# A two-layer gated cross-attention kernel: first-stage PSUM as four pairs of banks, a group's three score slots in a row

## The chip, the cores and the metric

One Trainium2 chip, one of its cores. The metric is device microseconds (us) for one launch of the whole program, lower is better. The program computes with TensorE (matrix products, here PE for its matmuls and PEld for its weight loads), VectorE (DVE), ScalarE (ACT) and GpSimd (POOL); SyncE (SP) issues most DMAs. Matrix products land in PSUM, eight banks of 512 float32 values in each of 128 partitions; only DVE and ACT read them out from there.

## The reference

All values are float32. Sixteen sequences `x` of 256 tokens by 256 features pass through two layers, each an attention to a context of 77 tokens and a feed-forward part, each added to `x` through a `tanh` gate:

```python
x = x + tanh(g_xattn[0]) * L0_xattn(ctx, layernorm(x))   # first stage: this change
x = x + tanh(g_ffn[0])   * L0_ffn(layernorm(x))          # second stage: 2 of 8 experts per token
x = x + tanh(g_xattn[1]) * L1_xattn(layernorm(x), ctx)   # third stage
x = x + tanh(g_ffn[1])   * L1_ffn(layernorm(x))          # fourth stage: gated linear attention
```

The first stage, cut to what matters:

```python
xl, l = layer_norm(ctx), layer_norm(layernorm(x))
q     = l @ Wq                                   # 16 heads of 64
k, v  = split(concat([xl, l], axis=1) @ Wkv)     # 256 + 77 = 333 keys
w     = softmax(q k^T / 8)
out   = (w v) merged over heads @ Wo
```

## The kernel before

The program runs the four stages one after the other. A check at the end decides whether a slow exact version is run as well; it isn't here. The change lies in `stage0_fast`, the first stage, and in two small steps of `Route`, the second stage's routing, which runs in between.

**Units.** `stage0_fast` works on 64 units `(b, g)`: 16 sequences, and for each four groups `g` of four heads. The engines follow the written order: the objects `pe`, `act`, `dve` and `pool` go through the class `Pinned`, whose `call` (line 50) keeps every instruction in its engine's program order. So nearly every row of the profile has line 50, and one tells rows apart by their tiles. The order of one unit is written out in the loop over `units`:

- `run(ahead_of, ...)`: small statistics and routing steps.
- `scores(b, g, ahead)`: 333 keys are three chunks of 111 (`KC`), and a group has two head pairs `n`, so there are six blocks. Three slots `sc`, each two banks, take two blocks each: eight matmuls a slot (`sc<-qk`), each over 64 contraction rows, that is half of the array's height, so that the two heads `j` of a pair run side by side. Each slot is followed by one `exp` on ACT (`e<-sc`, 111x1024). Ahead of the third slot, `heads(*ahead, 0)` puts half of the next unit's projections.
- `heads(b, g, n)`: the queries and keys of one head pair, in banks `q` and `k`, with all 128 rows and columns; ACT takes `q` out (`qk<-q`), DVE takes `k` out (`qk<-k`).
- in group 1, `turn(b + 1)` (transposes `tr`, taken out by DVE into `kvT`) and `project(b - 1)` (`proj`, taken out and added to `x` by DVE).
- `sums`: POOL adds the exponentials of the unit over the chunks (`es`) and into a running check (`esum`).
- `values(*behind)`: for the unit before, `den<-es,ones` (the softmax sums) and `o<-e,v`, both as four tiles of 32 columns side by side; then DVE takes the reciprocal (`rd<-den`) and multiplies (`oT<-o,rd`).
- `run(behind_values, ...)`: routing products `rank`, `rtr` (group 2) and `rt` (group 3).
- in group 2, `all_values(b + 1)`: six products `v<-wkv,kvT` of 111x512 per sequence (three chunks by two halves `h`). ACT takes out half 0, DVE half 1, each right behind its half's matmuls in the program.
- `heads(*ahead, 1)`: the other half of the next unit's projections; `tally()`.

**PSUM.** The score slots have a pool of their own (`f0psc`, two slots of two banks); all else takes single banks from a pool of four (`f012ps`, `shared_bank`), which stages 1 and 2 go on using. `Route.logits` and `Route.ranks` leave their 16 and 32 columns in PSUM until a later unit reads them (`exps`, `place`).

Each matmul of the program runs as two passes in the trace, so counts in the profile are double those in the code. A tile that is written again waits for those that still read what it held; the waits are set by the framework from the tiles that instructions touch.

Of the kernel before, what the change touches and what calls it, by code (L numbers as in the profile page):

```python
# [10 lines left out]
F32 = mybir.dt.float32  # L11
I32 = mybir.dt.int32
AF = mybir.ActivationFunctionType
ALU = mybir.AluOpType
AX = mybir.AxisListType
PSUM = bass.MemoryType.PSUM

P = 128
B, S, D = 16, 256, 256
# [54 lines left out]
def layers(ctx: ExitStack, tc: tile.TileContext, t, out, check):  # L74
# [11 lines left out]
    xs, cs = [None] * B, [None] * B  # L86
# [19 lines left out]
    ws1 = s1.enter_context(tc.tile_pool(name="s1w", bufs=1, side="right"))  # L106
# [19 lines left out]
    wo0 = load_w("wo0h" if fast else "wo0", 1024, D, w0)  # L126
# [237 lines left out]
    class Route:  # L364
# [26 lines left out]
        def logits(self, b, bank):  # L391
            ps, xnT = bank("rt"), self.xnT.pop(b)
            for i in range(2):
                for k in range(2):
                    pe.matmul(ps[:, 8 * i:8 * i + 8], xnT[:, k, i * P:(i + 1) * P], rw1[:, k, :],
                              start=k == 0, stop=k == 1)
            self.ps[b] = ps

        def exps(self, b):

# [64 lines left out]
        def ranks(self, b, bank):  # L465
            hs, h1, h2 = self.hs[b]
            ps = bank("rank")
            pe.matmul(ps[:, :16], before, hs[:, 0].rearrange("p i e -> p (i e)"), start=True, stop=True)
            pe.matmul(ps[:, 16:32], ones, hs[:, 1].rearrange("p i e -> p (i e)"), start=True, stop=True)
            self.ps[b] = ps  # L470

        def place(self, b):

# [45 lines left out]
                nc.sync.dma_start(out=by_expert(rows, e),  # L519
                                  in_=bc(zero, [P, n, D], 1))  # L520

    def stage0_fast(bank):
        with ExitStack() as sx:
            w1 = sx.enter_context(tc.tile_pool(name="f0w1", bufs=1, reuse_waits="tile"))
            w2 = sx.enter_context(tc.tile_pool(name="f0w2", bufs=2, reuse_waits="tile"))
            psc = sx.enter_context(tc.tile_pool(name="f0psc", bufs=2, space=PSUM, reuse_waits="tile"))
            esum, rsum = check["esum"], check["rsum0"]

            xn, cn, kvT, v, oT = {}, {}, {}, {}, {}
# [21 lines left out]

            def turn(b):
                kvT[b] = w2.tile([P, 2, NK], F32, tag="kvT", name="kvT")
                for k in range(2):
                    ps = bank("tr")
                    for i in range(2):
                        pe.transpose(ps[:, i * P:(i + 1) * P], xn[b][:, i, k * P:(k + 1) * P], ident)
                    pe.transpose(ps[:, S:NK], cn[b][:, 0, k * P:(k + 1) * P], ident[:S2, :S2])
                    dve.tensor_scalar(kvT[b][:, k, :S], ps[:, :S], vec[:, V_LN2G + k:V_LN2G + k + 1],
                                            vec[:, V_LN2B + k:V_LN2B + k + 1], ALU.mult, ALU.add)  # L560
                    dve.tensor_scalar(kvT[b][:, k, S:], ps[:, S:NK], vec[:, V_LN1G + k:V_LN1G + k + 1],
                                            vec[:, V_LN1B + k:V_LN1B + k + 1], ALU.mult, ALU.add)

            def all_values(b, *between):
                v[b] = w2.tile([KC, 3, 1024], F32, tag="v", name="v")
                for c in range(3):
                    for h in range(2):
                        ps = bank("v")
                        for k in range(2):
                            pe.matmul(ps[:KC, :], kvT[b][:, k, c * KC:(c + 1) * KC],  # L570
                                             wkv0[:, k, 1024 + h * 512:1024 + (h + 1) * 512],
                                             start=k == 0, stop=k == 1)
                        if h == 0:
                            act.copy(v[b][:, c, :512], ps[:KC, :])
                        else:
                            dve.tensor_copy(v[b][:, c, 512:], ps[:KC, :])
                    for x in between[c:c + 1]:
                        x()
# [3 lines left out]
            def heads(b, g, n):  # L582

                if n == 0:
                    qk[b, g] = w2.tile([P, 2, S + NK], F32, tag="qk", name="qk")
                m = 2 * g + n
                psq, psk = bank("q"), bank("k")
                for k in range(2):
                    pe.matmul(psq[:, :S], wq0[:, k, m * P:(m + 1) * P], kvT[b][:, k, :S], start=k == 0, stop=k == 1)
                for k in range(2):  # L590
                    pe.matmul(psk[:, :NK], wkv0[:, k, m * P:(m + 1) * P], kvT[b][:, k, :], start=k == 0, stop=k == 1)
                act.mul(qk[b, g][:, n, :S], psq[:, :S], 0.125)
                dve.tensor_copy(qk[b, g][:, n, S:], psk[:, :NK])

            def scores(b, g, between):

                x_qk = qk.pop((b, g))
                e = w2.tile([KC, 6, 2, S], F32, tag="e", name="e")
                for u in range(0, 6, 2):
                    if u == 4 and between is not None:  # L600
                        heads(*between, 0)
                    sc = psc.tile([P, 2, 2, S], F32, tag="sc", name="sc")
                    for x in range(2):
                        n, c = divmod(u + x, 3)
                        for j in range(2):
                            r = slice(64 * j, 64 * j + 64)
                            pe.matmul(sc[:KC, j, x, :], x_qk[r, n, S + c * KC:S + (c + 1) * KC],
                                             x_qk[r, n, :S], start=True, stop=True)
                    act.activation(e[:, u:u + 2], sc[:KC].rearrange("p j x s -> p x j s"), AF.Exp)
                return b, g, e  # L610
# [10 lines left out]
            def values(b, g, e, es):  # L621

                if g == 0:
                    oT[b] = w1.tile([P, 8, S], F32, tag="oT", name="oT")
                den, ps = bank("den"), bank("o")
                heads = [(h, slice(32 * h, 32 * h + 32)) for h in range(4)]
                for h, r in heads:
                    n, j = divmod(h, 2)
                    pe.matmul(den[r, :S], ones[:KC, :32], es[:, n, j * S:(j + 1) * S], start=True, stop=True)
                for i in range(2):  # L630
                    for c in range(3):
                        for h, r in heads:
                            n, j = divmod(h, 2)
                            lo = (4 * g + h) * 64 + 32 * i
                            pe.matmul(ps[r, i * S:(i + 1) * S], v[b][:, c, lo:lo + 32], e[:, 3 * n + c, j, :],
                                      start=c == 0, stop=c == 2)
                rd = w2.tile([P, S], F32, tag="rd", name="rd")
                dve.reciprocal(rd, den[:, :S])
                dve.tensor_tensor(oT[b][:, 2 * g:2 * g + 2, :], ps.rearrange("p (i s) -> p i s", i=2),
                                  bc(rd, [P, 2, S], 1), ALU.mult)  # L640
                tallies.append((rd, rsum[:, 4 * b + g:4 * b + g + 1]))
# [4 lines left out]
                tallies.clear()  # L646

            def project(b):
                for i in range(2):
                    ps = bank("proj")  # L650
                    for m in range(8):
                        pe.matmul(ps[:, :D], oT[b][:, m, i * P:(i + 1) * P], wo0[:, m, :],
                                         start=m == 0, stop=m == 7)
                    dve.scalar_tensor_tensor(xs[b][:, i, :], ps[:, :D], gate[:, 0:1], xs[b][:, i, :],
                                                   ALU.mult, ALU.add)


            ahead_of = {0: [(norm_y, 1), (route.exps, -2)], 1: [(route.choose, -2)],
# [26 lines left out]
            for n, (b, g) in enumerate(units):  # L685
                ahead = units[n + 1] if n + 1 < len(units) else None
                run(ahead_of, b, g)
                now = scores(b, g, ahead)
                if g == 0 and b + 2 < B:
                    load_c(b + 2)  # L690
                run(behind_scores, b, g)
                if b == 0 and g == 1:
                    clear_rows()
                if g == 1 and b + 1 < B:
                    turn(b + 1)
                if g == 1 and b > 0:
                    project(b - 1)
                now = sums(*now)
                if behind is not None:
                    values(*behind)  # L700
                run(behind_values, b, g)
                if g == 2 and b + 1 < B:
                    all_values(b + 1, *route.weighted(b - 2))
                if ahead is not None:
                    heads(*ahead, 1)
                if g == 2 and b + 1 == B:
                    pieces = route.weighted(b - 2)
# [17 lines left out]
            project(B - 1)  # L725

    if fast:
        s_banks = ctx.enter_context(ExitStack())
        pss = s_banks.enter_context(tc.tile_pool(name="f012ps", bufs=4, space=PSUM, reuse_waits="tile"))

        def shared_bank(name):
            return pss.tile([P, 512], F32, tag="ps", name=name)

        stage0_fast(shared_bank)
    else:
        stage0()
    s0.close()
# [1245 lines left out]
```

## Time and profile before

| what | value |
|---|---|
| time, median of 3 runs | 1972.6 us (1970.68 to 1974.86) |
| the profiled execution | 1979.72 us, span 1977.9 us, mean granted clock 0.988 |
| first stage in the span | up to the first expert matmul at 1004.5 us |
| PE busy in the span | 1936.2 us (98%) |
| PEld, DVE, ACT, POOL busy | 1314.5, 1050.2, 865.7, 1001.3 us |

The profile is one execution, some 7 us above the median of the timed runs. Busy time of PE says little by itself: its matmuls overlap, and the end of each is modelled. What one pass really costs is read from the start of one instruction to the start of the next. In the rows, `sc<-qk 64*111 64x256` reads: result tile `sc` from `qk`, weights of 64 rows by 111 columns, a moving operand of 256 columns.

### The profile page before, as it was taken

To read this page: it belongs to the slowest core of one execution; us is meant where nothing else is said; L and a number is where in the kernel's file an instruction comes from. 1 tells how busy PE (TensorE), PEld (TensorE's weight loads), DVE (VectorE), ACT (ScalarE), POOL (GpSimd) and SP (SyncE) were. 2 spreads that over 40 slices of the span, in tenths; PEclk is the share of its full clock that TensorE was granted. 3 is DMA by queue.
4 is the path that set the end of the run, shared out by engine and by line. 5 is a ranking of instruction groups with operands and counts; after the bars stand their busy time and mean duration, and the time that the engine had idled before them with its cause. 6 is when DMAs were issued, how large, how long until landed. Compare 5 with 4: busy or idle time off the path is not lost.

```text
span 1977.9 us, 35117 instructions
## 1 busy us (share of the span) xinstructions
PE 1936.2 (98%) x13986; PEld 1314.5 (66%) x13986; DVE 1050.2 (53%) x2651; ACT 865.7 (44%) x1763; POOL 1001.3 (51%) x905
## 2 busy tenths in 40 slices
PE   7999999999999999999989999999999999999996
PEld 4666666566665666656677766667777777777775
DVE  3334444444444444444454378866566665666654
ACT  3333334433344333443433478744444444444442
POOL 4544656556565565655634756214444444444433
PEclk9999999999999999999999989999999999999998
DMA  9400000000000000000068823000000000000000
GB/s 333 132 1 3 13 11 13 9 10 11 11 13 10 10 11 9 12 9 9 12 217 238 216 40 49 14 1 6 6 6 7 6 11 6 7 6 9 9 7 13
DMA packets 54013, 75.05 MB, mean 38 GB/s; under 512 B 10080, under 2 KB 43728, under 8 KB 53328
## 3 DMA queue, kind: packets, MB, share of 16 engines
q1 hardware_dynamic: 41552, 55.92, 8.5%
q0 software_dynamic: 12288, 16.79, 4.3%
q8 instruction: 113, 1.85, 0.4%
q14 instruction: 60, 0.49, 0.1%
HBM read 39.14 MB, written 33.55 MB: 37 GB/s over the span
## 4 chain that ended last, share of the span: by engine, by line
PE 95%; DVE 2%; ACT 1%; DMA 1%; POOL 1%; issue 1%; SPq 0%; ACTq 0%; DVEq 0%; POOLq 0%
PE o L50 11%; PE sc L50 11%; PE v L50 9%; PE q L50 8%; PE k L50 8%; PE proj L50 7%; PE kq L1508 6%; PE sc L1508 5%; PE gq L1508 3%; PE proj L1508 3%; PE v L1508 3%; PE ex L50 3%; PE o L1508 3%; PE den L50 2%; PE gz L1508 2%; PE z L1508 2%
## 5 line engine op out<-in xcount | busy, mean ns | idle before, releaser
L50 ACT ACTIVATE e<-sc 111x1024 f32<-111x1024 f32 x192 | 189.3, 1021 | 172.8 <-PE sc L50 172.7
L50 POOL TENSOR_SCALAR rs<-mv 128x2 f32<-128x2 f32 (+1 forms) x96 | 18.4, 192 | 434.3 <-DVE mv L50 431.6
L50 PE MATMUL sc<-qk 64*111 64x256 f32 x1536 | 198.6, 391 | 1.3 <-ACT qk L50 1.0
L50 POOL TENSOR_TENSOR es<-e 111x1024 f32<-111x1024 f32 x64 | 151.3, 2364 | 92.7 <-ACT e L50 92.6
L50 PEld LDWEIGHTS sc<-qk 64*111 64x111 f32 x1536 | 126.7, 172 | 79.0 <-issue 51.5
L50 PE MATMUL o<-e,v 111*32 111x256 f32 x3072 | 178.8, 381 | 0.0
L50 PE MATMUL v<-wkv,kvT 128*111 128x512 f32 x384 | 168.7, 596 | 0.1
L50 DVE COPY qk<-k 128x333 f32<-128x333 f32 x128 | 64.7, 505 | 194.8 <-PE k L50 192.7
L50 POOL TENSOR_TENSOR esum<-esum,es 111x512 f32<-111x512 f32 x128 | 163.0, 1273 | 10.0
L50 PE MATMUL k<-kvT,wkv 128*128 128x333 f32 x512 | 164.4, 443 | 0.0
L50 ACT ACTIVATE qk<-q 128x256 f32<-128x256 f32 x128 | 49.2, 385 | 260.5 <-PE q L50 259.9
L50 POOL TENSOR_TENSOR k<-e,ee 128x256 f32<-128x256 f32 x64 | 46.9, 733 | 223.9 <-ACT e L50 223.9
L50 POOL TENSOR_TENSOR es<-es,e 111x1024 f32<-111x1024 f32 x64 | 150.4, 2350 | 5.0
L50 PEld LDWEIGHTS o<-e,v 111*32 111x32 f32 x3072 | 100.5, 111 | 67.0 <-issue 1.7
L50 PE MATMUL q<-kvT,wq 128*128 128x256 f32 x512 | 142.6, 401 | 0.0
L50 DVE RECIPROCAL rd<-den 128x256 f32<-128x256 f32 x64 | 112.5, 1757 | 54.5 <-PE den L50 52.9
L50 POOL TENSOR_TENSOR at<-at,at 128x768 f32<-128x768 f32 x64 | 115.9, 1811 | 24.8 <-DVE at L50 15.2
L50 PEld LDWEIGHTS v<-wkv,kvT 128*111 128x111 f32 x384 | 66.9, 177 | 90.6 <-issue 86.4
L50 DVE TENSOR_TENSOR at<-sc,amask 128x768 f32<-128x768 f32 x64 | 61.3, 957 | 115.8 <-PE sc L1508 100.4
L50 PEld LDWEIGHTS q<-kvT,wq 128*128 128x128 f32 x512 | 88.2, 189 | 50.0 <-issue 43.2
L50 PEld LDWEIGHTS k<-kvT,wkv 128*128 128x128 f32 x512 | 97.2, 190 | 30.0
L50 POOL DMA_INDIRECT x<-rows_out,pos x64 | 100.4, 1568 | 32.2 <-issue 15.9
(228 smaller groups left out, 4092.4 us busy)
## 6 DMA issues: line engine op xcount, KB each, us to landing
rows<-zero SPq DMA_DIRECT2D x16, 640.0 KB
xin<-rows SPq DMA_DIRECT2D x16, 640.0 KB
rows_out<-y SPq DMA_DIRECT2D x16, 384.0 KB
x<-in_x_dram SPq DMA_DIRECT2D x16, 256.0 KB
rows_out<-y SPq DMA_DIRECT2D x16, 256.0 KB
out_dram<-x SPq DMA_DIRECT2D x16, 256.0 KB
wkv<-in_wkv_dram SPq DMA_DIRECT2D x2, 1024.0 KB
ew<-in_ew_dram SPq DMA_DIRECT2D x2, 1024.0 KB
```

What stands on the lines that cost most here:

```text
L50: x = getattr(self.engine, name)(*a, **k)
L1508: tc.keep_in_program_order(nc.tensor.matmul(*a, **k))
```

## The change

- `stage0_fast` gets a pool of its own, `f0ps`, of four pairs of banks; every step takes a whole pair (`pair`), and `bank` is the first half of one. The shared pool of four banks is made after the stage.
- The three score slots stand one behind the other; `heads(*ahead, 0)` goes to the end of the unit, right ahead of `heads(*ahead, 1)`. `values(*behind)` comes directly behind the scores, and `turn` and `project` behind it.
- `heads`, `values`, `turn`, `project` and `all_values` each put two results into the halves of one pair. `turn` and `project` now run all their matmuls first and take out afterwards, `project` with one DVE instruction in place of two. In `all_values` ACT's copy of half 0 still stands between the matmuls of half 0 and half 1.
- `Route.logits` and `Route.ranks` copy their columns into SBUF with ACT (`copied`), so that no pair is held.

```diff
+            self.copied(b, ps[:, :16])          # logits; ranks: ps[:, :32]
+        def copied(self, b, ps):
+            n = ps.shape[1]
+            self.ps[b] = ws1.tile([P, n], F32, tag=f"copied{n}", name="copied")
+            act.copy(self.ps[b], ps)
...
-            psc = sx.enter_context(tc.tile_pool(name="f0psc", bufs=2, space=PSUM, reuse_waits="tile"))
+            pairs = sx.enter_context(tc.tile_pool(name="f0ps", bufs=4, space=PSUM, reuse_waits="tile"))
+            def pair(name):
+                return pairs.tile([P, 2, 512], F32, tag="ps", name=name)
+            def bank(name):
+                return pair(name)[:, 0, :]
...
             def turn(b):
+                both = pair("tr")
                 for k in range(2):
-                    ps = bank("tr")
+                    ps = both[:, k, :]
                     for i in range(2):
                         pe.transpose(ps[:, i * P:(i + 1) * P], xn[b][:, i, k * P:(k + 1) * P], ident)
                     pe.transpose(ps[:, S:NK], cn[b][:, 0, k * P:(k + 1) * P], ident[:S2, :S2])
+                for k in range(2):
+                    ps = both[:, k, :]
                     dve.tensor_scalar(kvT[b][:, k, :S], ...)
...
             def all_values(b, *between):
                 for c in range(3):
+                    both = pair("v")
                     for h in range(2):
-                        ps = bank("v")
+                        ps = both[:, h, :]
                         for k in range(2):
                             pe.matmul(ps[:KC, :], kvT[b][:, k, c * KC:(c + 1) * KC], ...)
                         if h == 0:
                             act.copy(v[b][:, c, :512], ps[:KC, :])
                         else:
                             dve.tensor_copy(v[b][:, c, 512:], ps[:KC, :])
...
             def heads(b, g, n):
-                psq, psk = bank("q"), bank("k")
+                both = pair("qk")
+                psq, psk = both[:, 0, :], both[:, 1, :]
...
-            def scores(b, g, between):
+            def scores(b, g):
                 for u in range(0, 6, 2):
-                    if u == 4 and between is not None:
-                        heads(*between, 0)
-                    sc = psc.tile([P, 2, 2, S], F32, tag="sc", name="sc")
+                    sc = pair("sc").rearrange("p j (x s) -> p j x s", x=2)
...
             def values(b, g, e, es):
-                den, ps = bank("den"), bank("o")
+                both = pair("o")
+                den, ps = both[:, 0, :], both[:, 1, :]
...
             def project(b):
-                for i in range(2):
-                    ps = bank("proj")
+                both = pair("proj")
+                for i in range(2):
                     for m in range(8):
-                        pe.matmul(ps[:, :D], ...)
-                    dve.scalar_tensor_tensor(xs[b][:, i, :], ps[:, :D], gate[:, 0:1], xs[b][:, i, :], ...)
+                        pe.matmul(both[:, i, :D], ...)
+                dve.scalar_tensor_tensor(xs[b], both[:, :, :D], gate[:, 0:1], xs[b], ALU.mult, ALU.add)
...
-                now = scores(b, g, ahead)
+                now = scores(b, g)
...
+                now = sums(*now)
+                if behind is not None:
+                    values(*behind)
                 if g == 1 and b + 1 < B:
                     turn(b + 1)
                 if g == 1 and b > 0:
                     project(b - 1)
-                now = sums(*now)
-                if behind is not None:
-                    values(*behind)
                 run(behind_values, b, g)
                 if g == 2 and b + 1 < B:
                     all_values(b + 1, *route.weighted(b - 2))
                 if ahead is not None:
+                    heads(*ahead, 0)
                     heads(*ahead, 1)
```

More of the change, by code (lines that the diff above doesn't have):

```diff
@@ L396, in logits @@
                               start=k == 0, stop=k == 1)
-            self.ps[b] = ps
+            self.copied(b, ps[:, :16])
[3 more added lines that the diff above has]
+            act.copy(self.ps[b], ps)
         def exps(self, b):
@@ L469, in ranks @@
             pe.matmul(ps[:, 16:32], ones, hs[:, 1].rearrange("p i e -> p (i e)"), start=True, stop=True)
-            self.ps[b] = ps
+            self.copied(b, ps[:, :32])
         def place(self, b):
@@ L520, in clear_rows, with stage0_fast @@
                                   in_=bc(zero, [P, n, D], 1))
-    def stage0_fast(bank):
+    def stage0_fast():
         with ExitStack() as sx:
@@ L648, in project @@
             def project(b):
+                both = pair("proj")
                 for i in range(2):
-                    ps = bank("proj")
                     for m in range(8):
-                        pe.matmul(ps[:, :D], oT[b][:, m, i * P:(i + 1) * P], wo0[:, m, :],
+                        pe.matmul(both[:, i, :D], oT[b][:, m, i * P:(i + 1) * P], wo0[:, m, :],
                                          start=m == 0, stop=m == 7)
-                    dve.scalar_tensor_tensor(xs[b][:, i, :], ps[:, :D], gate[:, 0:1], xs[b][:, i, :],
-                                                   ALU.mult, ALU.add)
+                dve.scalar_tensor_tensor(xs[b], both[:, :, :D], gate[:, 0:1], xs[b], ALU.mult, ALU.add)
             ahead_of = {0: [(norm_y, 1), (route.exps, -2)], 1: [(route.choose, -2)],
@@ L727, in layers @@
     if fast:
+        stage0_fast()
         s_banks = ctx.enter_context(ExitStack())
@@ L732, in shared_bank @@
             return pss.tile([P, 512], F32, tag="ps", name=name)
-        stage0_fast(shared_bank)
     else:
```

## The prediction

> **What bounds the kernel now.** I read the profile's chain of waits first, to see which engine sets the end.
>
> ```profile
> PE 95%; DVE 2%; ACT 1%; DMA 1%; POOL 1%; issue 1%; SPq 0%; ACTq 0%; DVEq 0%; POOLq 0%
> ```
>
> PE carries it, and the waits between 100 and 950 us name no wait of PE at all, only of the engines that feed on it. So in the first stage each step costs what PE takes from its start to the start of the next, and whatever makes PE wait is added in full. The timeline of PE gives those steps (start, modelled length, passes):
>
> ```profile
> 497.03 1.03 PE L50 MATMUL q<-kvT,wq 128*128 128x256 f32 x4
> 497.90 1.28 PE L50 MATMUL k<-kvT,wkv 128*128 128x333 f32 x4
> ...
> 501.03 1.13 PE L50 MATMUL q<-kvT,wq 128*128 128x256 f32 x4
> 502.00 1.28 PE L50 MATMUL k<-kvT,wkv 128*128 128x333 f32 x4
> 503.21 1.12 PE L50 MATMUL sc<-qk 64*111 64x256 f32 x8
> 504.26 0.64 PE L50 MATMUL den<-es,ones 111*32 111x256 f32 x8
> ...
> 510.49 1.98 PE L50 MATMUL sc<-qk 64*111 64x256 f32 x16
> 512.41 1.13 PE L50 MATMUL q<-kvT,wq 128*128 128x256 f32 x4
> ...
> 957.75 7.17 PE L50 MATMUL proj<-wo0h,oT 128*128 128x256 f32 x32
> 964.85 0.64 PE L50 MATMUL den<-es,ones 111*32 111x256 f32 x8
> ```
>
> The same four `q` passes take 0.87 us behind `v` (497.03 to 497.90, both of the full array) and 0.97 behind scores (501.03 to 502.00). Score passes: x16 take 1.92, x8 take 1.05, so eight cost 0.87 and each run of scores carries 0.18 more, however long it is. PE pays where the shape of its tiles changes.
>
> **The change, part by part.**
>
> *Scores together, heads 0 moved to the unit's end.* One run of 24 passes for runs of 16 and 8 saves one fixed 0.18. The `q` of the second `heads` call now follows `k`, full shape behind full shape: 0.10. The `k` of the first no longer goes over to scores: it took 502.00 to 503.21 = 1.21; the `v` row below gives 10.30 us for 24 passes of 512 columns, 0.84 ns a column, so four passes of 333 are 1.12, and 0.09 goes. Together 0.37 in each of the 63 units that have a next one: 23.3 us.
>
> *Turn and project behind the values.* Before, this block stood alone between scores and `den`. 32 `proj` passes took 957.75 to 964.85 = 7.10, against 32 x 256 x 0.84 ns = 6.87. Behind the values and ahead of `heads` it changes shape no more often than the unit does anyhow: 0.2 x 16 = 3.2 us. Saved in all: **26.5 us**.
>
> *`all_values` with both halves in one pair.* This part decides. The changed program as it is built shows the waits: in every `v` pair the first matmul of half 1 waits for ACT's copy of half 0, since both halves are now one tile and the copy stands ahead of that matmul. Before, the halves were two tiles, and PE ran all 24 passes of a sequence without a break while ACT and DVE took out:
>
> ```profile
> 486.73 10.46 PE L50 MATMUL v<-wkv,kvT 128*111 128x512 f32 x24
> 488.65 0.59 ACT L50 COPY v<-v 111x512 f32<-111x512 f32 x1 [1.13 <-PE v L50]
> ```
>
> 24 passes from 486.73 to 497.03 are 0.43 each. Half 0 is four passes; the fourth starts at 488.02, ends at 488.61 (a `v` pass lasts 0.592) and releases the copy at 488.65. It is done at 489.24. How long PE takes to restart behind ACT, this place shows:
>
> ```profile
> 982.75 1.94 ACT L50 ACTIVATE e<-sc 111x1024 f32<-111x1024 f32 x2 [0.67 <-PE sc L50]
> 983.83 1.12 PE L50 MATMUL sc<-qk 64*111 64x256 f32 x8 [0.32 <-ACT e L50]
> ```
>
> The first of the two `exp` (1.02 each) ends at 983.77, the matmul starts at 983.83: 0.06. So half 1 starts at 489.30 where it started at 488.45: 0.85 late, plus a weight load that nothing covers, 0.10 (the 0.18 of the score run restarted here has to be such a load and the change of shape at its end). 0.95 x 3 pairs x 16 sequences = **45.6 us**. Bounds: 0.85 if the load is covered (40.8), 1.05 if PE needs another 0.1 for the wait (50.4); below nothing is excluded, as the copy cannot start before half 0 ends. Queued behind PE's wait is everything, since PE is the chain. ACT is free for each copy: the two `xw` behind it take 0.91 and the next half 0 ends over 4 us later.
>
> *`heads` in one pair.* ACT's `qk<-q` now waits for the last `k` pass, and DVE's `qk<-k` for ACT: 0.39 + 0.51 + about 0.1 behind the end of `k`. Both are done about 1.5 us after the last `k` pass starts. The first matmul that needs head pair 1 is the seventh of the twelve: 0.37 (change of shape) + 0.95 + 0.43 = 1.75 after it, with its weight load some 0.2 sooner. It just fits: 0. Missed by 0.1 it would cost 63 x 0.1 = 6.3, the upper bound; it cannot gain.
>
> *`values` in one pair.* The reciprocal (1.76) now waits for the last `o` pass, not for `den`, and `oT` (0.69) follows: the pair is free 2.6 us after `o`. PE then has at least the two `heads` (4.2 us) to do, and the next to need that pair is the second score slot. In group 1 `oT` also waits for `project(b - 1)`, which still reads the one `oT` buffer, so DVE stands for 7 us with `kvT`, `x` and both `qk` copies behind it. Afterwards it needs 0.69 + 1.78 + 0.75 + 0.51, done 3.7 us behind `proj`, when PE is still in `heads` (4.2 us). Cover: `heads`. 0.
>
> *`es` on POOL.* `den` comes some 2.6 us sooner behind the scores of the unit before. In the unit at 504 us `es` ended at 510.3 and `den` started at 515.64; 5.3 of slack become 2.7. 0; were it gone, each us would be paid 64 times.
>
> *Copies of 16 and 32 columns, one `x` update for two.* Two small ACT copies a sequence (the small `re<-re` is 0.22) in gaps where ACT waits for PE; DVE's 0.75 (the `128x512` form of that operation later in the run) for 2 x 0.48. Off the chain: 0. SP and POOL issue the same first-stage transfers in the same order; a few loads of the second stage change place on SP, 0 with 1 us either way.
>
> *Start.* The two first `heads` and the first `turn` run with nothing to cover their longer take-out (0.44 and twice 0.2): 0.7 us.
>
> Sum: -26.5 + 45.6 + 0.7 = **+19.8 us**. Against the profiled execution, 1979.7 becomes 1999.5; its time is 7.1 above the median of the timed runs, so the forecast for these is 1972.6 + 19.8 = **1992.4**.
>
> A rule weighed here: the Trainium skill's page "PSUM — Partial Sum Buffer", in its summary of rules, asks only that a reader and a running matmul be in different banks. By it the halves of a pair could go on side by side, and the sum would be -25.8, 1946.8. But the wait is set by tile and is carried in the program, so the trace's durations decide.
>
> **The rivals.**
>
> *Faster: the half-1 wait costs little.* Then the shape changes alone count: 1972.6 - 26.5 + 0.7 = 1946.8. For it: nothing on the chip needs the wait. Against: the copy's 0.59 lies wholly behind half 0. The point of decision is 26.5 / 48 = 0.55 us a half; above that the kernel is slower. I see no way below 0.85. Chance 0.04.
>
> *The clock drops.* An idle PE is given half the clock for a stretch of 3.41 us. Rows of such stretches (length, PE busy and count, weight loads, DVE, ACT, POOL, then the granted clock):
>
> ```profile
> 28.81:32.22 3.41, 2.71 (x20) 2.08 (x21) 1.13 (x5) 2.46 (x5) 0.88 (x2) 1.00 0.99 394
> 32.22:35.63 3.41, 3.41 (x19) 2.21 (x18) 0.64 (x3) 1.61 (x3) 0.00 (x0) 1.00 1.06 337
> 1308.81:1312.22 3.41, 2.37 (x17) 1.75 (x16) 2.45 (x8) 0.75 (x1) 0.28 (x2) 1.00 0.00 0
> 1312.22:1315.64 3.42, 3.42 (x11) 2.76 (x10) 3.16 (x5) 0.00 (x0) 0.61 (x1) 0.50 0.00 0
> 1947.11:1950.52 3.41, 2.55 (x24) 1.77 (x20) 3.23 (x7) 0.95 (x2) 0.73 (x1) 1.00 0.23 79
> 1950.52:1953.93 3.41, 2.96 (x16) 1.73 (x18) 1.83 (x5) 1.89 (x5) 2.61 (x3) 1.00 0.00 0
> ```
>
> 1.04 idle in a stretch brought 0.50 in the next; 0.70 and 0.86 did not. The new gap is 488.61 to 489.30 = 0.69 by the same reckoning, and gaps come 4.4 us apart, so a stretch holds one at most. Below the point, but not by much. If it tips, about 38 of the 48 gaps lie whole in a stretch, each costs half of 3.41: 38 x 1.7 = 65 more, 2057. Chance 0.10. The Trainium skill's "TensorE: Matmul & The Clock Gate" speaks more darkly of this change: under its second failure mode, short idle spells between groups of matmuls, as PSUM banks are cycled, keep the clock swinging, while its table of advice fears only gaps above about 3 us. The first would make it the 2057, the second the 1992.
>
> *No gain from the order.* If the shape changes cost as much in the new places: 1972.6 + 45.6 + 0.7 = 2018.9. Against it: the 0.87 of `q` behind `v`. Chance 0.03.
>
> **How the numbers follow.** The forecast has 0.81, the clock 0.10, no gain 0.03, the faster rival 0.04, a result within 0.2% (about 4 us, what a measurement can tell from no change) 0.02. The forecast's own ends: 40.8 - 30 (0.05 more saved per unit) = +10.8, so 1983; 50.4 + 6.3 + 2 - 23.3 = +35.4, so 2008. Range 1983 to 2008, which leaves out the clock case, no gain and the faster one. Slower: 0.81 + 0.10 + 0.03 = 0.94.
>
> **What would show it.** Right: `sc<-qk` in runs of 24 at about 2.78 us, `q` behind `k` at 0.87; in `v`, a gap of 0.85 to 1.05 after every fourth pass, named as a wait of PE for ACT's `v`, some 33 us idle in all (48 x 0.69); the first expert matmul some 20 us later; clock 1.00 up to there. Wrong: `v` still 10.3 us a sequence; stretches of 0.50 in the `v` phases; waits of `sc` for `qk` or of `den` for `es`.

## The result, and the profile after

| | us, median | ratio to the kernel before, 95% interval |
|---|---|---|
| before, same chip | 1973.7 (1970.68 to 1980.31) | |
| after | 2002.3 (1998.81 to 2008.06) | 1.0143 [1.0106, 1.0180] |
| forecast | 1992.4 (1983 to 2008) | 1.0100 |

The kernel is slower by 28.6 us where 19.8 were forecast. The profiled execution took 2008.06 us, span 2006.3, against 1979.72 and 1977.9 before: 28.4 more. The chain of waits still says that PE sets the end, with 90% where it had 95%:

```profile
PE 90%; DVE 3%; ACT 3%; POOL 2%; issue 1%; DMA 1%; SPq 0%; ACTq 0%; POOLq 0%; DVEq 0%
```

The waits of PE between 100 and 950 us (total, times, longest) were empty before. Now there are two:

```profile
PE v L50 <- ACT v L50: 28.4, 42, 0.7
PE rtr L50 <- ACT rxn L50: 1.2, 2, 1.1
```

42 times is three for each of the 14 sequences in the window. The timeline of PE shows the place, and, some lines further, the shape changes that were saved:

```profile
499.48 1.88 PE L50 MATMUL v<-wkv,kvT 128*111 128x512 f32 x4
502.03 3.69 PE L50 MATMUL v<-wkv,kvT 128*111 128x512 f32 x8 [0.68 <-ACT v L50]
506.40 3.69 PE L50 MATMUL v<-wkv,kvT 128*111 128x512 f32 x8 [0.68 <-ACT v L50]
510.76 1.97 PE L50 MATMUL v<-wkv,kvT 128*111 128x512 f32 x4 [0.68 <-ACT v L50]
512.57 1.03 PE L50 MATMUL qk<-kvT,wq 128*128 128x256 f32 x4
513.43 1.28 PE L50 MATMUL qk<-kvT,wkv 128*128 128x333 f32 x4
514.55 1.02 PE L50 MATMUL qk<-kvT,wq 128*128 128x256 f32 x4
515.41 1.28 PE L50 MATMUL qk<-kvT,wkv 128*128 128x333 f32 x4
516.63 2.85 PE L50 MATMUL sc<-qk 64*111 64x256 f32 x24
519.40 0.64 PE L50 MATMUL o<-es,ones 111*32 111x256 f32 x8
...
544.30 7.11 PE L50 MATMUL proj<-wo0h,oT 128*128 128x256 f32 x32
551.25 1.03 PE L50 MATMUL qk<-kvT,wq 128*128 128x256 f32 x4
```

In program order the 24 passes of a sequence used to be one block of 10.30 us. They are now four blocks with a gap of 0.68 behind every half 0, from 499.48 to 512.57 = 13.09. The 24 score passes are one run, 516.63 to 519.40 = 2.77 (2.78 forecast). `q` behind `k` takes 514.55 to 515.41 = 0.86 (0.87). `proj` takes 6.95 where it took 7.10. What releases each block is ACT's copy:

```profile
501.40 0.58 ACT L50 COPY v<-v 111x512 f32<-111x512 f32 x1 [1.13 <-PE v L50]
501.88 0.91 ACT L50 ACTIVATE xw<-rxn,rw 128x256 f32<-128x256 f32 x2
502.03 0.27 PEld L50 LDWEIGHTS v<-wkv,kvT 128*111 128x111 f32 x2 [1.52 <-ACT v L50]
```

The copy ends at 501.98. The weight load and the matmul of half 1 start at 502.03, 0.05 later. PEld had stood for 1.52: the load waits with its matmul, so nothing covers it.

From sequence to sequence (`v` to `v`, sequences 6 to 15) the kernel takes 62.71 us where it took 61.66, so 1.05 more. That is +2.785 for the three gaps and -1.735 for the order.

### The profile page after: what moved, and what is told of

It is laid out like the page before. It is cut to its first block, busy times and chain, and to the rows that moved or that the text cites. A ratio compares the mean times of both kernels' runs of the same rounds, so it can differ in the third digit from the quotient of the medians.

```text
span 2006.3 us, 34963 instructions
## 1 busy us (share of the span) xinstructions
PE 1925.8 (96%) x13986; PEld 1324.0 (66%) x13986; DVE 1090.7 (54%) x2635; ACT 868.8 (43%) x1795; POOL 1001.5 (50%) x905
## 3 DMA queue, kind: packets, MB, share of 16 engines
q8 instruction: 112, 1.84, 0.4%
## 4 chain that ended last, share of the span: by engine, by line
PE 90%; DVE 3%; ACT 3%; POOL 2%; issue 1%; DMA 1%; SPq 0%; ACTq 0%; POOLq 0%; DVEq 0%
PE o L50 13%; PE qk L50 13%; PE sc L50 10%; PE v L50 9%; PE proj L50 7%; PE kq L1525 6%; PE sc L1525 5%; PE gq L1525 3%; PE proj L1525 3%; PE v L1525 3%; PE o L1525 3%; PE ex L50 2%; PE gz L1525 2%; PE z L1525 2%; PE den L1525 1%; PE q L50 1%
## 5 line engine op out<-in xcount | busy, mean ns | idle before, releaser
L50 PE MATMUL v<-wkv,kvT 128*111 128x512 f32 x384 | 184.2, 617 | 33.1 <-ACT v L50 32.4
L50 ACT ACTIVATE qk<-qk 128x256 f32<-128x256 f32 x128 | 49.1, 384 | 379.5 <-PE qk L50 379.5
L50 ACT ACTIVATE e<-sc 111x1024 f32<-111x1024 f32 x192 | 182.2, 1021 | 17.8 <-PE sc L50 17.8
L50 PE MATMUL sc<-qk 64*111 64x256 f32 x1536 | 182.2, 383 | 1.6 <-DVE qk L50 1.6
L50 DVE RECIPROCAL rd<-o 128x256 f32<-128x256 f32 x64 | 112.3, 1755 | 103.6 <-PE o L50 103.6
L50 PE MATMUL qk<-kvT,wkv 128*128 128x333 f32 x512 | 164.3, 443 | 0.0
L50 DVE COPY qk<-qk 128x333 f32<-128x333 f32 x128 | 64.6, 505 | 134.5 <-ACT qk L50 133.1
L50 PE MATMUL qk<-kvT,wq 128*128 128x256 f32 x512 | 134.3, 385 | 0.0
L50 DVE COPY v<-v 111x512 f32<-111x512 f32 x48 | 33.2, 692 | 169.5 <-PE v L50 169.5
L50 PEld LDWEIGHTS qk<-kvT,wkv 128*128 128x128 f32 x512 | 97.2, 190 | 30.0
```

The lines of the kernel that those rows point to most:

```text
L50: x = getattr(self.engine, name)(*a, **k)
```

## The experiments

All ratios are to the kernel before on the same chip (medians of it 1972.5 to 1973.8). "Per sequence" is `v` to `v` in the profile, "at the experts" is the start of the first expert matmul against 1004.49 before.

| kernel | us | ratio, interval | per sequence | at the experts |
|---|---|---|---|---|
| before | | | 61.66 | 0 |
| after | 2002.3 | 1.0143 [1.0106, 1.0180] | 62.71 | +24.4 |
| after, again | 2001.5 | 1.0123 [1.0090, 1.0156] | 62.71 | +27.4 |
| matmuls of both halves first | 1950.8 | 0.9871 [0.9840, 0.9903] | 59.92 | -23.2 |
| a pair for each half | 1954.4 | 0.9916 [0.9884, 0.9949] | 59.92 | -20.2 |
| before, halves in one tile | 2017.1 | 1.0207 [1.0176, 1.0237] | 64.45 | +44.5 |
| after, one-off places out | 1999.3 | 1.0130 [1.0111, 1.0150] | 62.75 | +21.2 |
| matmuls first, one-offs out | 1949.6 | 0.9879 [0.9864, 0.9894] | 59.96 | -21.0 |
| after, copy twice | 2026.9 | 1.0280 [1.0257, 1.0303] | 64.56 | +50.4 |
| after, copy four times | 2096.2 | 1.0655 [1.0560, 1.0749] | 68.26 | +118.6 |
| before, scores together | 1999.9 | 1.0143 [1.0126, 1.0160] | 63.45 | +26.0 |
| matmuls first, `heads` between | 1978.7 | 1.0025 [1.0008, 1.0042] | 61.54 | +2.2 |
| matmuls first, turn ahead | 1956.5 | 0.9918 [0.9894, 0.9943] | 60.12 | -19.1 |

### The kernel after, once more

> The changed kernel once more, for the 8.8 us by which it was slower than the sum (28.6 measured, 19.8 forecast). Theory (one-off places): the sum's steady part is right, 2.79 us of wait less 1.74 saved, +1.05 a sequence; the rest came from three places, each once in a launch: a wait of rtr for rxn near 181 us with a stretch of half clock behind it (+4.6), the last den of the first stage (+2.7), one wait of ex in the second stage (+4.4). Then it stays at +24 to +29 against the kernel before and the profile shows +1.05 a sequence again; those of the three places that are set by timing alone may be absent. Rival (spread): the pairs cost a little everywhere, then the sequences differ by more than 1.05 each.

Measured: 62.71 per sequence again, gaps of 0.68 again. At the experts it is 3.0 later than the first profile; the granted clock is full from 22.86 us on there and from 16.27 in the first, and half of that 6.6 is 3.3. So some 3 us of difference between two profiles are the start alone. The expected third place, a wait of `ex` behind the stage, did not come back: from the first expert matmul to the end it took 974.2 us here, 977.4 in the first profile and 973.4 before.

### Both halves' matmuls ahead of both copies

```diff
-                    for h in range(2):
-                        ps = both[:, h, :]
-                        ... matmuls of half h; then act.copy (h == 0) or dve.tensor_copy (h == 1)
+                    for h in range(2):
+                        ... matmuls of half h into both[:KC, h, :]
+                    act.copy(v[b][:, c, :512], both[:KC, 0, :])
+                    dve.tensor_copy(v[b][:, c, 512:], both[:KC, 1, :])
```

> all_values runs the matmuls of both halves first and takes out afterwards, the rest as in the changed kernel. Theory (the wait on the own pair): the 0.68 us gaps in v go, v falls from 13.09 to 10.30 us a sequence, 44.6 us in all; 2002 becomes about 1957 with the three one-off places, 1949 without. Rival (no gain from the order): then it lands near the kernel before, 1973, or above. Rival (clock): if the gaps cost clock as well, it falls by clearly more than 44.6.

```profile
474.95 10.46 PE L50 MATMUL v<-wkv,kvT 128*111 128x512 f32 x24
...
478.58 0.58 ACT L50 COPY v<-v 111x512 f32<-111x512 f32 x1 [2.85 <-PE v L50]
...
479.20 0.69 DVE L50 COPY v<-v 111x512 f32<-111x512 f32 x1 [2.44 <-ACT v L50]
...
485.25 1.03 PE L50 MATMUL qk<-kvT,wq 128*128 128x256 f32 x4
```

The timeline of this kernel: one block of 10.30 us again. The tile is still shared: DVE's copy starts as ACT's ends (479.16); in the kernel before, with two tiles, it waited for PE alone. But that chain, 1.3 us, hangs behind a pair that nobody needs soon, and no longer between two matmuls. 1950.8 us, 23 less than the kernel before: the whole change but for the place of one line. That lies between the two times expected; the wait of `rtr` for `rxn`, described below, stands in this trace too, but no half clock follows it.

### A pair of its own for each half

```diff
-                    both = pair("v")
                     for h in range(2):
-                        ps = both[:, h, :]
+                        ps = bank("v")
```

> Each half of v takes a pair of its own again (half of it unused), copies between the matmuls as in the changed kernel. Theory: the wait is set by the tile, not by where the copy stands; with two tiles it goes, and the time is that of e2, 1949 to 1957, v 10.30 us a sequence. Rival (too few pairs): six pairs in a rotation of four make PE wait for the take-out of v itself, DVE's being the slow one; then v stays above 10.30 and the time lies between e2 and the changed kernel.

```profile
477.37 10.46 PE L50 MATMUL v<-wkv,kvT 128*111 128x512 f32 x24
487.67 1.03 PE L50 MATMUL qk<-kvT,wq 128*128 128x256 f32 x4
```

The copy stands between the halves as in the kernel after, but the halves are two tiles: 10.30 us a sequence, no wait of PE in `v` between 100 and 950 us. So it is neither ACT's copy nor its place alone that costs, but both together with the one tile.

### The kernel before, with the halves in one tile

```diff
+                    both = psc.tile([P, 2, 512], F32, tag="sc", name="v")
                     for h in range(2):
-                        ps = bank("v")
+                        ps = both[:, h, :]
```

> The kernel before, with one part of the change alone: the two halves of v as one tile of two banks (taken from the score slots), copies where they stand. Theory: 48 waits of 0.93 us and nothing saved, 1973 + 44.6 = 2018, v 13.09 us a sequence. Rival (the wait needs the new rotation of pairs): then 1973. Rival (clock): above 2040.

The waits of PE between 100 and 950 us, all of them:

```profile
PE v L50 <- ACT v L50: 26.3, 39, 0.7
```

39 is three for each of the 13 sequences whose `v` lies in that window. 64.45 - 61.66 = 2.79 per sequence, 0.93 a gap, 44.6 in 16 sequences; 44.5 at the experts. The wait alone, without the new order, costs that.

### The two terms of the order, one at a time

`heads(*ahead, 0)` back ahead of the third score slot, in the version with the matmuls first:

> Both halves' `v` matmuls ahead of both copies, four pairs of banks, and the first `heads` of the next unit back ahead of the third score slot, as in the kernel before. Theory (the order saves shape changes, 0.37 in each of 63 units): +23.3 against the same version with the score slots together, so about the time of the kernel before, ratio 0.998 to 1.002, score runs of 16 and 8. Rival (the gain of that version comes from the pairs or from turn and project): ratio 0.987.

```profile
501.22 1.98 PE L50 MATMUL sc<-qk 64*111 64x256 f32 x16
503.14 1.13 PE L50 MATMUL qk<-kvT,wq 128*128 128x256 f32 x4
504.11 1.28 PE L50 MATMUL qk<-kvT,wkv 128*128 128x333 f32 x4
505.32 1.12 PE L50 MATMUL sc<-qk 64*111 64x256 f32 x8
```

`q` behind scores takes 0.97 again, the runs 1.92 and 1.05. 61.54 - 59.92 = 1.62 per sequence, 0.40 a unit where 0.37 was forecast: 25.5 in 63 units. The time is 28 above the version with the slots together, and 0.25% above the kernel before; the expected 0.2% at most lies within the interval.

`turn` and `project` back ahead of the values:

> Both halves' `v` matmuls ahead of both copies, four pairs of banks, scores together, but turn and project back ahead of the values, as in the kernel before. Theory (0.2 of shape change in each of 16 sequences): +3.2 against the version with them behind the values, up to +4.5 if all of the saving beyond the first term (27.8 - 23.3) lies here; ratio 0.9885 to 0.9895, and 0.2 to 0.28 more from `v` to `v`, 59.92 becoming 60.12 to 60.20. Rival (no shape change is saved there): 59.92 a sequence, ratio 0.987.

60.12 - 59.92 = 0.20 per sequence, as forecast, 3.2 in all. The measured time lies 5.7 above, more than was forecast; the ratio's interval reaches the forecast (0.9885 to 0.9895) only at its lower end. So the 0.20 is shown by the trace and not by the timed runs. The two terms sum to 1.82 a sequence, while the version with the matmuls first gains 1.74 on the kernel before; 0.08 was not located.

### The order on the old banks

The score slots keep a pool of two slots, and only `heads(*ahead, 0)` goes to the unit's end (turn and project stay, and the 16 and 32 columns are copied):

```diff
-                    if u == 4 and between is not None:
-                        heads(*between, 0)
...
+                    heads(*ahead, 0)
                     heads(*ahead, 1)
```

> The kernel before with its own PSUM pools, and only the first `heads` of the next unit moved from between the score slots to the unit's end (and the 16 and 32 columns copied, so that no bank is held); turn and project stay where they were. Theory (shape changes saved: 0.37 x 63 = 23.3; but the third slot has to wait for the first `exp`, since the scores have two slots of their own: 0.32 idle, as in the last unit of the kernel before, plus a weight load of 0.1, x 63 = 26.5): +3, ratio 1.0 to 1.003, with a wait of `sc` for ACT's `e` of about 0.3 in every unit. Rival (the wait is covered, the order alone brings the gain): -23, 0.988. Then the four pairs would not be needed for it.

```profile
523.60 1.98 PE L50 MATMUL sc<-qk 64*111 64x256 f32 x16
...
525.76 0.22 ACT L50 ACTIVATE re<-re 128x16 f32<-128x16 f32 x1 [2.40 <-DVE re L50]
...
525.88 1.92 ACT L50 ACTIVATE e<-sc 111x1024 f32<-111x1024 f32 x2
...
526.94 1.12 PE L50 MATMUL sc<-qk 64*111 64x256 f32 x8 [1.36 <-ACT e L50]
```

Slower than expected, 26 us and not 3. In three units of four the third slot waits about the expected 0.32 for the first `exp`. In group 0 it waits 1.36, because on ACT the routing's `re<-re` stands ahead of that `exp` and has itself waited for DVE. With two slots the scores hang on ACT's queue. So on the old banks the order costs more than it saves; with the four pairs it pays, but the pairs bring the tile that both halves of `v` share, if one isn't careful.

### Two one-off places

The trace of the kernel after has two more places where PE loses time, once each. In the third sequence (timeline, then windows of one clock stretch each: length, PE, PEld, DVE, ACT, POOL busy, granted clock):

```profile
178.35 0.70 POOL L50 TENSOR_TENSOR rs<-rs,nhalf 128x2 f32<-128x2 f32 x1
179.01 2.37 POOL L50 TENSOR_TENSOR es<-e 111x1024 f32<-111x1024 f32 x1
179.09 2.31 DVE L50 SCALAR_TENSOR_TENSOR rs<-mv,rs 128x2 f32<-128x2 f32 x1 [1.10 <-POOL rs L50]
...
180.41 0.40 PE L50 MATMUL rank<-hs,before 128*128 128x16 f32 x2
...
181.44 1.09 ACT L50 ACTIVATE rxn<-x,rs 128x256 f32<-128x256 f32 x2 [2.87 <-DVE rs L50]
...
182.09 0.33 PE L50 MATMUL rtr<-ident,rxn 128*128 128x128 f32 x1 [1.07 <-ACT rxn L50]
```

```profile
180.11:183.53 3.42, 2.19 (x18) 1.36 (x11) 3.39 (x3) 1.52 (x4) 3.34 (x2) 1.00 0.00 0
183.53:186.94 3.41, 2.73 (x5) 0.59 (x4) 0.26 (x1) 1.10 (x3) 2.82 (x3) 0.50 0.00 0
186.94:190.36 3.42, 3.42 (x5) 1.25 (x6) 0.00 (x0) 0.51 (x2) 0.00 (x0) 0.50 0.00 0
```

A DVE instruction on two columns, which takes 0.15 elsewhere, lasts 2.31: it starts 0.08 behind POOL's `es` and ends with it. `rxn` and `rtr` follow, PE idles 1.07 and then has half the clock for 6.83. In later sequences a scatter stands on POOL between `rs` and `es`. Before the change POOL waited 2.21 for the `exp` there, and `rs` was done long before `es` began; with the scores together that `exp` comes sooner. Sequence 2 to 5 takes 7.7 us longer than before where 3.1 would be the steady loss: 4.6. At the end of the stage the last `den` (in the kernel after a half of tile `o`) waits longer for POOL's `es`. First the kernel before, then the kernel after:

```profile
991.30 1.06 PE L50 MATMUL den<-es,ones 111*32 111x256 f32 x8 [2.21 <-POOL es L50]
```

```profile
1014.82 1.08 PE L50 MATMUL o<-es,ones 111*32 111x256 f32 x8 [3.19 <-POOL es L50]
```

6.83 us of half clock follow, where 3.41 did before: 0.98 + 1.71 = 2.7.

Both were taken out of the kernel after:

```diff
-            behind_values = {2: [(route.ranks, -2, bank), (route.turn, -1, bank)], ...}
+            behind_values = {2: [(route.ranks, -2, bank)], ...}
...                                       # behind all_values(b + 1, ...)
+                if g == 2 and b > 0:
+                    route.turn(b - 1, bank)
...                                       # last unit only: now = sums(*now) ahead of run(behind_scores, b, g)
```

> The kernel after with two one-off places taken out: `rtr` stands behind the `v` products instead of ahead of them, and in the last unit POOL's `es` sums stand ahead of the scatter. Theory (the 8.8 us that the forecast missed lie in these two places): the 1.07 us that PE waits for `rxn` in the third sequence go, and with them the half clock of 6.83 us behind it (3.4): -4.5; `den` of the last unit starts 0.99 earlier, and with an idle time of 2.2 in place of 3.19 perhaps one stretch of half clock less (1.7): -1.0 to -2.7. Sum -5.5 to -7.2, so +21 to +23 against the kernel before, a ratio of 1.0107 to 1.0118; the `v` phases stay at 13.09 us a sequence. Rival (the extra is spread over the units, or differs from execution to execution): no change against the kernel after, +28, 1.0125 to 1.0145.

The trace agrees with the theory. The wait for `rxn` is gone, and sequence 2 to 5 is 5.0 shorter. The last `den` waits 2.35 and one stretch of half clock follows. At the experts the kernel is 6.2 ahead of the second profile of the kernel after, whose clock became full at nearly the same time (22.48 and 22.86). The timed runs, 1.0130 [1.0111, 1.0150], can't tell it from the kernel after: 26.0 us above the kernel before, where that one had 28.6 and 27.7.

The same edits on the version with the matmuls first:

> Both halves' `v` matmuls ahead of both copies (10.30 us a sequence, as run before), with the same two one-off places taken out. Theory: the wait for `rxn` had no half clock behind it here, so 1.06 goes, and 0.99 to 2.7 at the stage's end: -2.0 to -3.8 against that version without the two edits, that is -25 to -27 against the kernel before, 0.9863 to 0.9873. Rival (the two places are covered again by the next wait): -23, 0.988.

1949.6 against 1950.8: no difference can be told, and with 23.6 less than the kernel before the rival's 23 fits better than the theory's 25 to 27. The wait for `rxn` is gone here too, but the 2.13 that PE idles ahead of the first scores, as in the version without the two edits, had a stretch of half clock behind it this time. Both versions beat both kernels.

### What it takes to lower the clock

ACT's copy of half 0 done twice, in the kernel after:

```diff
                         if h == 0:
                             act.copy(v[b][:, c, :512], ps[:KC, :])
+                            act.copy(v[b][:, c, :512], ps[:KC, :])
```

> The kernel after, with ACT's copy of half 0 of `v` done twice, so that PE's gap between the halves grows from 0.68 to about 0.68 + 0.58 = 1.26 us, above the 1.04 of idle time that was followed by half the clock in the kernel before. If only the wait counts: +0.58 x 48 = 28 against the kernel after, +56 against the one before, about 2030, ratio 1.028, clock still 1.00 in the `v` phases. If idle time above about 1.04 in a stretch of 3.41 us halves the clock of the next: most of the 48 gaps lie in one stretch, each brings up to 1.7 more, 50 to 80 in all, 2080 to 2110, ratio 1.054 to 1.07, with 0.50 in the rows of the `v` phases.

Gaps of 1.29 us, 64.56 per sequence (1.85 more, 0.62 a gap), 2026.9 us against "about 2030" without the clock, and full clock throughout `v`. One stretch that holds a whole gap, and the next:

```profile
457.80:461.21 3.41, 2.12 (x6) 0.74 (x5) 0.13 (x1) 1.97 (x4) 0.00 (x0) 1.00 0.00 0
461.21:464.63 3.42, 3.42 (x15) 2.38 (x14) 0.78 (x2) 0.38 (x1) 0.00 (x0) 1.00 0.00 0
```

PE idled 1.29 in the first and kept the full clock in the second. The prediction's point of 1.04 idle was wrong. Four copies:

> The kernel after, with ACT's copy of half 0 of `v` done four times. With the copy done twice the gap was 1.29 us, 0.61 more, and the clock stayed at 1.00; here it should be about 2.5. Theory (the clock of a stretch of 3.41 us falls when the work that PE streams in the stretch before it, columns by 0.84 ns, is below about 1.45 us, and idle time counts only as far as it lowers this): the stretches that hold a whole gap stream some 0.8 us, so half the clock follows behind most of the 48 gaps; 2 x 0.61 x 48 = 58.6 for the gaps against the version with two copies, and 1.0 to 1.7 a gap for the clock, 48 to 82 more: 2133 to 2167, ratio 1.081 to 1.098, with 0.50 in the `v` phases. Rival (the granted clock does not answer to gaps between matmuls of one phase at all): only the 58.6, about 2085, ratio 1.057, clock 1.00 up to the end of the stage.

Windows of one clock stretch each of that kernel:

```profile
141.77:145.18 3.41, 1.03 (x3) 0.18 (x1) 0.12 (x1) 2.25 (x4) 0.00 (x0) 1.00 0.00 0
145.18:148.59 3.41, 3.26 (x4) 1.38 (x5) 0.00 (x0) 0.10 (x1) 0.00 (x0) 0.50 0.00 0
414.83:418.24 3.41, 1.57 (x4) 0.80 (x5) 0.00 (x0) 2.53 (x5) 3.25 (x3) 1.00 0.00 0
418.24:421.65 3.41, 2.12 (x5) 0.53 (x3) 0.69 (x1) 1.19 (x3) 0.50 (x1) 1.00 0.00 0
```

Gaps of 2.5 us: the clock does fall, but in this execution only four times among the gaps, and not once after 210 us. The reason seems to be an accident of length: a sequence takes 68.26 us here, which is 20 stretches of 3.413, so the gaps come to lie in the same position in every sequence, split between two stretches. The three executions behind the ratio took 2089.7, 2096.2 and 2116.1 us at mean granted clocks of 0.990, 0.987 and 0.978; a fourth, left out of it, took 2129.4 at 0.972. The number lies between theory and rival, and the theory's count of drops was wrong.

Its rule fits better than idle time. By idle time the stretches are in the wrong order: the one at 414.83 above was idle for 1.84 and kept the full clock, the one at 180.11 in the kernel after for 1.23 and lost it. Now count the columns that PE streams in a stretch (0.84 ns each, divided by the tiles that run side by side, spread over the length of their pass in the trace). The first stages of all thirteen profiles here sort like this: from full clock, half clock followed where 1.34 us or less of 3.41 was streamed, and full clock stayed with 1.45 or more. Between them both occurred (1.38 stayed, 1.43 fell), and another way to place the columns within a pass moves these bounds by some 0.1. The stretch at 180.11 streamed about 1.2, although PE counts as busy for 2.19 of it: the `rank` passes are busy but stream 16 columns each. In the kernel with two copies a stretch with a whole gap of 1.29 streamed at least 1.8. The rule was read off these traces and was not tested on a kernel built for it.

## Why the prediction was right or wrong

Right: the sign, the mechanism, and the two large terms. In the sum of the profiled executions:

| term | forecast | measured |
|---|---|---|
| half 1 waits for ACT's copy | +45.6 (0.95 each) | +44.6 (0.93 each) |
| shape changes saved | -26.5 | -27.8 (1.735 x 16) |
| start | +0.7 | +0.3 |
| third sequence: `rtr` waits for `rxn`, half clock | not seen | +4.6 |
| end of the stage: `den` waits for `es`, half clock | 0 | +2.7 |
| behind the stage | 0 (1 either way) | +4.0 |
| sum | +19.8 | +28.4 |

The wait is shown from both sides: 2.79 per sequence with it alone, none with the tile split or the copy moved. Of the saving, `heads` was mis-sized by a little (0.40 a unit, not 0.37).

**The step that failed** is "`es` on POOL ... 0". Its slack was counted in the steady units, and there it held. It did not ask what else meets an earlier `es`: in the third sequence DVE's `rs`, at the end of the stage a last `den` that had no slack even before (it waited 2.21). The prediction looked for a wait in every unit, and what it missed came once each. These two terms are read from the profiles; the timed runs without the two places can't confirm their size. That the range held the result all the same is partly luck: its upper end was made of a slower restart, the pair of `heads` and the transfers, and none of these is what the kernel lost. The 4.0 behind the stage is not a cost of the change that the runs show: the time from the first expert matmul to the end was 966.6 to 977.4 in the profiles of all these kernels, whose code is the same there, and the first profile of the kernel after had the 977.4, the one before 973.4.

Heads serial, the wait of `oT`, the copies, the order on SP: forecast at 0, and between 100 and 950 us no wait of PE for any of them stands in the trace.

**The rivals.** "The half-1 wait costs little" gave 1946.8; with the wait taken out the kernel measured 1950.8, so the rival's sum was sound and only its condition was missing. "The clock drops" was refuted for this change with room to spare, and for another reason than the prediction had: not because 0.69 is below 0.86 but, by the rule above, because a stretch that holds such a gap still streams 2.3 us or more, far above 1.45. The Trainium skill's "TensorE: Matmul & The Clock Gate" fears, under its second failure mode, that short idle spells between groups of matmuls make the clock swing; gaps of 0.68 and of 1.29, three a sequence, never did here. Its table fears only gaps above some 3 us, yet half the clock followed 1.07 of idle time at 181 us. "No gain from the order" falls with the runs that undo its two parts.

## What to carry to other kernels

When two results are put into one tile, look at every reader that stands between their writers in the program: each becomes a wait, whatever the banks allow. Issue all the writers first and the readers behind them, or give each its own tile; here this one move turned +28 us into -23. And when a change makes an engine's step earlier, check the places that occur once (first sequences, last unit) as well as the steady loop.

## What the runs showed of the hardware

- DVE instructions with two inputs in SBUF waited here until a large `tensor_tensor` of POOL had ended. In the first stage of the kernel after, `rs<-mv,rs` took 0.15 to 0.16 in 62 cases and 2.31 in the one that began under an `es`; `rq<-p,m` took 0.17 outside of POOL's sums and 0.94 when begun inside, ending 0.03 behind POOL's instruction each time. `oT<-o,rd` (0.69), copies and reductions, which read PSUM or one SBUF operand, took the same inside and outside. The Trainium skill's "SBUF — State Buffer", under "Who interferes with whom", says that a DVE instruction with two SBUF inputs contends with a GpSimd instruction that reads SBUF; the trace agrees.
- A change of shape in PE's tiles, going to the scores' 64 rows from full rows and back for another run of eight, cost 0.40 us a unit, and the order of the steps alone removed it.
- In these traces the granted clock went with what PE streamed in a stretch of 3.41 us rather than with how long it idled: a stretch with 1.84 us idle kept full speed, one with 1.23 beside products of 16 columns did not. No kernel was built to test this.
